# Four graph-attention layers on one core: new table rows stored from ScalarE's queue, and the smallest tile processed last

## The chip, the cores and the metric

The kernel runs on one core of a Trainium2 chip, with no other core at work. The metric is device time in microseconds, the median of repeated executions. One further execution was recorded by the hardware profiler; all durations, waits and times of day below come from that one. The engines are named as the profile names them: PE (TensorE), DVE (VectorE), ACT (ScalarE), POOL (GpSimd) and SP (SyncE), whose only work here is to issue transfers. PEld is the loading of weights into TensorE.

## The reference: what is computed

There are 3327 nodes with 512 features each, and one adjacency matrix with few entries. Four layers follow each other. Each normalises the rows of x (layer norm), applies ReLU, computes graph attention over the neighbours of every node, and adds the result to x:

```
h = relu(layernorm(x));  x = x + GAT_l(h, adj)          # l = 0, 1, 2, 3

GAT_l:  Wh = h @ W_l                                    # 512 -> 512, as 8, 4, 1, 8 heads
        s, d = Wh . a_src, Wh . a_dst                   # one number per node and head
        e[i, j] = leaky_relu(s[i] + d[j]), only where adj[i, j] > 0
        out[i] = sum_j softmax_j(e[i, :])[j] * Wh[j]    # elu on it in layers 1 and 2
```

## The kernel before

**Preparation.** The adjacency matrix is turned once into a list of neighbours for every node. Nodes are ranked by their number of neighbours and cut into 26 tiles of 128 nodes: tile 0 holds the nodes with the most neighbours, tile 25 those with the fewest. `CAPS` gives the number of neighbour slots of each tile: 36 for tile 0, 25 for tile 1, 23 for tile 2, 19 for tile 9, 12 for tile 24, 11 for tile 25. The lists themselves (`idxa` for tiles 18 to 25, `idxb` for the others) stay in SBUF.

**Tables.** For each layer there is a table in HBM with a row of 528 floats for each node: Wh and the attention numbers. Layer 0 reads `tabx`, made in the preparation. Later layers read `tabs[l % 2]` while they write `tabs[(l + 1) % 2]`, the table of the layer after.

**Steps.** A tile of a layer is done in steps of up to four slots (`GROUP`). For one step:
- `Tile.fetch` gathers one neighbour row for each of 128 nodes per slot, by an indirect DMA that POOL issues (L830, `g<-tab`). The node's own row is slot 0 and comes by a plain load from SP (L861); in layer 0 it comes with a gather of double width.
- `Tile.scored` computes the weights: two small operations on DVE (L883, L885, tile `z`), then Exp on ACT (L886, tile `pw`).
- `Tile.group` multiplies the four gathered rows by their weights on DVE (L912, tile `m`), and PE adds them up in PSUM (L917, tile `bank`, two matmuls per slot). In layer 2, with one head, DVE does both by itself (L905 and L907).

`steps` is the list of all steps of a layer, tile after tile in the order of the list `order`, which counts down from 25: the tile with the fewest slots comes first. Gathers are issued `LOOK` = 7 steps ahead. Tile indices below `DENSE[l]` (0, 1, 9 and 2 in the four layers) are left out of this list. They are done by dense attention over all nodes instead (classes `Several` and `Wholes`), in units that are spread evenly over the steps, up to eight before the last. Their loads (L1094, L1096, L1225, L1226) come from SP.

**The end of a tile.** After a tile's last step, `finish` and `ends` put the pieces that remain at fixed distances behind it: the divisors (L922 to L924), the mean (L934, in layer 2 L930), elu (`bent`, L940 and L942), the addition to x (L954), then for the next layer the centring (`xn`, L962, and its squares, L965), the root (L970, L435 to L441, in layer 2 on POOL, L432), the turn by four transposes (L451), ReLU (`hT`, L458), the projection of 16 matmuls (L469, tile `pv`, one PSUM buffer), and last `rows`: ACT copies the scaled result to `v` (L476, three buffers), and SP stores it in the next layer's table (L988, `tab<-v`). There are 78 such stores, one for each tile of layers 0 to 2.

**Order on the engines.** On PE, DVE, ACT and POOL the instructions stand in the order in which the code emits them; nothing passes a waiting instruction. On SP a scheduler sets the order of the transfers. The first gather of a layer waits until all rows of its table have been stored.

**The end of layer 0.** Between the last eight steps, and after them, stand 26 steps of class `Ranked`: each gathers mask rows (POOL, `spare<-found`) into one of three buffers and stores them again, sorted (SP, L1056, `masks<-spare`), for the dense parts of the later layers. Nine further steps of class `Mask` are inserted at fixed numbers earlier in layer 0. `Weights` loads a later layer's matrix (L394, `w<-in_w`, two transfers of 512 KB).

Of the kernel before, what the change touches and what calls it, by code (L numbers as in the profile page):

```python
# [18 lines left out]
P = 128  # L19
# [454 lines left out]
def scaled(nc, pv, rstd, work):  # L474
    v = work.tile([P, ROW], F32, name="v", bufs=3)
    nc.scalar.activation(v.rearrange("p (s n) -> p s n", s=2), pv[:, :, :ROW // 2], AF.Copy, scale=rstd)  # L476
    return v
# [47 lines left out]
def tile_gat_stack(ctx: ExitStack, tc: tile.TileContext, x, adj, adjT, ws, avs, out):  # L525
# [261 lines left out]
    with cond.Else():  # L787
        tile_gat_lists(tc, x, adj, ws, avs, out, ident, half, slots, L, low, spare, tabx, tabs)
# [3 lines left out]
def tile_gat_lists(ctx: ExitStack, tc: tile.TileContext, x, adj, ws, avs, out, ident, half, slots, L, low, spare, tabx, tabs):  # L792
# [7 lines left out]
    nc = tc.nc  # L800
    NP, F = x.shape
    NT = NP // P
# [32 lines left out]
    def scatter():  # L835
        while waiting:
            dst, t, rows = waiting.pop(0)
            nc.gpsimd.indirect_dma_start(out=dst, out_offset=bass.IndirectOffsetOnAxis(ap=slots(t, 0), axis=0),  # L838
                                         in_=rows, in_offset=None)

    class Tile:
# [143 lines left out]
        def rows(self):  # L985
            if self.W is not None:
                v = scaled(nc, self.pv, self.rstd, work)
                nc.sync.dma_start(tabs[(self.l + 1) % 2][self.t * P:(self.t + 1) * P, :], v)  # L988

        def ends(self, s):  # L990

# [54 lines left out]
    class Ranked:  # L1046
# [5 lines left out]
        def fetch(self):  # L1052
            n = ND * P // 4
            rows = spare[:, self.j % 3 * n:(self.j % 3 + 1) * n].bitcast(I32)
            gather(rows, found, slots(self.j, 0))
            nc.sync.dma_start(masks[:, self.j, :, :].rearrange("s p c -> p s c"),  # L1056
                              rows.rearrange("p (s c) -> p s c", c=wide // 4))
# [259 lines left out]
    def later(s, place, piece):  # L1317
# [2 lines left out]
    out_v = dram_disjoint_views(out, NT)  # L1320
    ctx.enter_context(tc.manual_schedule(engines={mybir.EngineType.Pool, mybir.EngineType.PE,
                                                  mybir.EngineType.DVE, mybir.EngineType.Activation}))
    order = list(reversed(range(NT)))
    ys = itertools.cycle([low[:, 3 * F:4 * F], low[:, 4 * F:5 * F]])
    W = None
    following = Weights(nc, wpool, work, 1, ws, avs)
# [112 lines left out]
```

## Time and profile before

| | |
|---|---|
| median of 3 runs | 2492.9 us (2492.3 to 2494.5) |
| the profiled execution, whole / its span | 2493.66 us / 2491.9 us |
| busy: PE, DVE, POOL, ACT | 2083.4, 1935.6, 1710.7, 911.6 us (84%, 78%, 69%, 37%) |
| gathers and scatters on POOL | about 0.95 us each |
| preparation ends, first steps of layer 0 | about 320 us |
| first gather of layer 1 | 944.5 us |
| first gather of layer 2 | 1502.0 us |
| first gather of layer 3 | 1966.4 us |
| last output scatter | 2483.9 us |

The busy times overlap: each is the time in which that engine worked, whatever the others did. What a layer costs is read from the engine that has no gaps in it, and what a boundary between layers costs is read from the time between the last gather of one layer and the first of the next. In lines of groups, "m<-g,pw" is the output tile and the inputs; "x1304 | 810.6, 681" is the number of instructions, their busy time in us and the mean duration of one in ns; behind the second bar stands how long the engine was idle just before them, and what ended that. In lines of the timeline the first number is the start and the second the duration, both in us; the bracket at the end holds the idle time before and what ended it.

### The profile page before, as it was taken

The page shows a single profiled execution, that of the slowest core. Times are in us where ns is not written, and L with a number is a line of the kernel's source. Part 1 is how long each engine was busy: PE and PEld are TensorE (multiplying, and loading weights), DVE is VectorE, ACT ScalarE, POOL GpSimd, SP SyncE. Part 2 cuts the span into 40 slices and gives each one's busy share as a digit, 9 for nine tenths or more (in the row PEclk, how much of TensorE's full clock was granted, in tenths as well). Part 3 has the DMA queues.
Part 4 walks back from the last instruction along what each step waited for, and adds up shares of the span by engine and source line. Part 5 has one row for each costly group of instructions (what it writes and reads, how often), then busy time and mean ns, then how long its engine had stood idle before and what let it go on. Part 6 is the DMA issues. An engine that isn't in the chain of part 4 may idle for free. (4 is left out here: it accounts for less than half of the span.)

```text
span 2491.9 us, 26810 instructions
## 1 busy us (share of the span) xinstructions
PE 2083.4 (84%) x6832; PEld 1163.5 (47%) x6832; DVE 1935.6 (78%) x5004; ACT 911.6 (37%) x2506; POOL 1710.7 (69%) x1700
## 2 busy tenths in 40 slices
PE   3776789999898855999999986869696699999897
PEld 1655445555444422555555543434353454455453
DVE  7887787887767735788888876978979488787776
ACT  4777123343321102433333323433333343333330
POOL 7798367777777756776777746655546377777775
PEclk9888899999999987999999998979898899999999
DMA  6797579999887777877888858867777488888885
GB/s 231 280 298 240 173 219 291 284 298 296 277 270 237 231 194 239 261 244 228 247 258 258 252 162 264 271 194 239 211 229 212 134 253 247 246 250 250 240 243 173
DMA packets 262490, 599.55 MB, mean 241 GB/s; under 512 B 103923, under 2 KB 121331, under 8 KB 257974
## 3 DMA queue, kind: packets, MB, share of 16 engines
q0 software_dynamic: 126128, 438.08, 57.7%
q1 hardware_dynamic: 132454, 152.86, 19.2%
q10 hardware_dynamic: 3744, 6.82, 0.8%
q8 instruction: 55, 0.90, 0.1%
q14 instruction: 109, 0.89, 0.1%
HBM read 547.96 MB, written 49.65 MB: 240 GB/s over the span
## 5 line engine op out<-in xcount | busy, mean ns | idle before, releaser
L917 PE MATMUL bank<-m,ident 128*128 128x512 f32 x2608 | 1204.6, 608 | 132.6 <-DVE m L912 132.0
L912 DVE TENSOR_TENSOR m<-g,pw 128x512 f32<-128x512 f32 x1304 | 810.6, 681 | 137.3 <-ACT pw L886 131.5
L830 POOL DMA_INDIRECT g<-tab,idxb x734 | 698.2, 951 | 284.7 <-issue 173.1
L917 PEld LDWEIGHTS bank<-m,ident 128*128 128x128 f32 x2608 | 483.3, 193 | 714.0 <-issue 347.5
L469 PE MATMUL pv<-w,hT 128*128 128x264 f32 x1664 | 438.5, 420 | 67.4 <-ACT hT L458 38.8
L886 ACT ACTIVATE pw<-z 128x32 f32<-128x32 f32 (+5 forms) x434 | 84.0, 194 | 987.2 <-DVE z L885 987.1
L469 PEld LDWEIGHTS pv<-w,hT 128*128 128x128 f32 x1664 | 340.3, 208 | 170.3 <-ACT hT L458 44.1
L830 POOL DMA_INDIRECT g<-tabx,twiceb x342 | 324.2, 948 | 105.1 <-issue 78.6
L830 POOL DMA_INDIRECT g<-tab,idxa x297 | 283.6, 955 | 145.1 <-issue 78.2
L1133 PE MATMUL whole<-ve,em 128*128 128x512 f32 x468 | 222.4, 623 | 41.4 <-DVE em L1119 38.5
L883 DVE TENSOR_TENSOR z<-g,pw 128x32 f32<-128x32 f32 (+5 forms) x434 | 74.9, 173 | 189.3 <-DMA g<-tab,idxa 83.0
L683 POOL TENSOR_TENSOR key<-a,keys 128x3328 int32<-128x3328 int32 (+1 forms) x29 | 189.1, 6525 | 14.5 <-DVE cand L692 11.8
L907 DVE SCALAR_TENSOR_TENSOR bank<-g,pw,bank 128x512 f32<-128x512 f32 x243 | 183.2, 754 | 6.8
L1133 PEld LDWEIGHTS whole<-ve,em 128*128 128x128 f32 x468 | 90.1, 199 | 152.3 <-issue 90.7
L692 DVE MAX8 cand<-key 128x8 f32<-128x208 int32 x416 | 143.7, 363 | 0.1
L830 POOL DMA_INDIRECT g<-tabx,twicea x99 | 94.4, 954 | 67.8 <-issue 32.7
L451 PE MATMUL pt<-ident,xn 128*128 128x128 f32 x416 | 68.6, 291 | 85.5 <-ACT hT L458 31.0
L451 PEld LDWEIGHTS pt<-ident,xn 128*128 128x128 f32 x416 | 53.6, 149 | 122.6 <-issue 48.4
L1108 ACT ACTIVATE r<-low,mc,b 128x384 f32<-128x384 f32 x78 | 52.6, 674 | 153.5 <-DVE em L1119 116.6
L432 POOL TENSOR_TENSOR rstd<-ve,half 128x1 f32<-128x1 f32 x52 | 31.8, 611 | 107.3 <-DVE ve L970 61.7
L1242 ACT ACTIVATE r<-low,spare 128x256 f32<-128x256 f32 x208 | 98.9, 476 | 5.1
L885 DVE SCALAR_TENSOR_TENSOR z<-z 128x32 f32<-128x32 f32 (+5 forms) x434 | 78.8, 182 | 15.3 <-DVE z L883 0.4
(175 smaller groups left out, 2111.5 us busy)
## 6 DMA issues: line engine op xcount, KB each, us to landing
a<-in_adj SPq DMA_DIRECT2D x25, 1664.0 KB, 9.0
tab<-v SPq DMA_DIRECT2D x78, 264.0 KB, 4.0
ve<-tab SPq DMA_DIRECT2D x78, 264.0 KB, 4.5
g<-tab SPq DMA_DIRECT2D x66, 264.0 KB, 4.7
tabx<-vx SPq DMA_DIRECT2D x26, 528.0 KB, 9.5
g<-tab,idxb POOLq DMA_INDIRECT x734, 3.9
low<-tab SPq DMA_DIRECT2D x52, 132.0 KB, 3.4
room<-tab SPq DMA_DIRECT2D x52, 132.0 KB, 3.6
```

What stands on the lines that cost most here:

```text
L451: nc.tensor.transpose(pt[:, k, :], xn[:, k * P:(k + 1) * P], ident)
L469: nc.tensor.matmul(pv[:, s, :HF + 8], hT[:, k, :], W.w[:, k, s, :], start=(k == 0), stop=(k == KC - 1))
L683: nc.gpsimd.tensor_tensor(key[:, c:c + quarter], a[:, c:c + quarter], keys[:, c:c + quarter], OP.mult)
L692: nc.vector.max(cand[:, g * 8:(g + 1) * 8], key[:, g * SEG:(g + 1) * SEG])
L830: nc.gpsimd.indirect_dma_start(out=out_, out_offset=None, in_=table, in_offset=bass.IndirectOffsetOnAxis(ap=which, axis=0))
L885: nc.vector.scalar_tensor_tensor(z, z, SLOPE, z, OP.mult, OP.max)
L886: nc.scalar.activation(self.wt[:, k0:k0 + n, :H], z, AF.Exp)
L907: nc.vector.scalar_tensor_tensor(acc, v, w, acc, OP.mult, OP.add)
L912: nc.vector.tensor_tensor(m[:, q, :].rearrange("p (s h d) -> p s h d", s=2, d=D), v.rearrange("p s (h d) -> p s h d", d=D), wt[:, k0 + q, ...
L917: nc.tensor.matmul(self.po, ident, m[:, q, :], start=(k0 + q == 0), stop=(k0 + q == K - 1))
L1133: nc.tensor.matmul(tl.po.rearrange("p (s m) -> p s m", s=2), e[:, q * P:(q + 1) * P], v.rearrange("p (s m) -> p s m", s=2)[:, :, :F // 2], ...
L1242: nc.scalar.activation(self.r[:, h, :], self.a[:, g, :], AF.Relu, bias=-1.0, scale=self.b[:, j, g:g + 1])
```

## The change

There are two edits. The store of the new rows is issued from ScalarE's queue, directly behind the instruction that makes `v`, in place of SP's. And the order of the tiles in every layer becomes 24, 23, ..., 0, 25: the tile with the fewest slots moves from the head of the list to its end. Tiles that are done densely in a layer are left out of it as before.

```diff
         def rows(self):
             if self.W is not None:
                 v = scaled(nc, self.pv, self.rstd, work)
-                nc.sync.dma_start(tabs[(self.l + 1) % 2][self.t * P:(self.t + 1) * P, :], v)
+                nc.scalar.dma_start(tabs[(self.l + 1) % 2][self.t * P:(self.t + 1) * P, :], v)
...
-    order = list(reversed(range(NT)))
+
+    order = [*reversed(range(NT - 1)), NT - 1]
```

## The prediction

> **What bounds the kernel now.** I read the group list first, then the busy times by stretch, the waits of POOL and SP, and last the timeline around each of the three places where one layer ends and the next begins.
>
> From the group list and the DMA issues of the page:
>
> ```profile
> L830 POOL DMA_INDIRECT g<-tab,idxb x734 | 698.2, 951 | 284.7 <-issue 173.1
> ...
> tab<-v SPq DMA_DIRECT2D x78, 264.0 KB, 4.0
> ```
>
> A gather takes 0.95 us of POOL and is followed by 0.30 us before the next: one neighbour row per node every 1.25 us. Busy time by stretch (columns: PE, PEld, DVE, ACT, POOL busy with counts, clock, DMA share, GB/s):
>
> ```profile
> 1200.00:1470.00 270.00, 265.30 (x834) 144.71 (x833) 231.49 (x617) 97.84 (x283) 202.40 (x214) 1.00 0.83 251
> 1470.00:1502.00 32.00, 23.39 (x73) 13.71 (x71) 13.26 (x42) 6.25 (x14) 0.02 (x1) 0.95 0.17 49
> 1502.00:1700.00 198.00, 148.84 (x420) 80.47 (x421) 161.01 (x301) 77.70 (x218) 120.95 (x128) 0.89 0.78 244
> ```
>
> 214 POOL instructions by 1.25 us are 267.5 of 270 us: late in layer 1 the gathers fill the time, with PE (265.3) close behind. Layers 0 and 3 look alike. In layer 2 DVE leads (161 of 198 us). Between layers POOL does nothing: the next layer's gathers read the whole table, so the first waits for the last new row. The waits, of all engines and of SP's queue (total, times, longest):
>
> ```profile
> POOL g L830 <- DMA tab<-v: 40.6, 2, 32.7
> ...
> SPq L988 <- ACT v L476: 444.4, 70, 28.4
> ```
>
> The three boundaries in the timeline; 0 to 1, then 1 to 2, then 2 to 3:
>
> ```profile
> 917.71 0.70 ACT L476 ACTIVATE v<-pv,rstd 128x528 f32<-128x528 f32 x1 [5.61 <-PE pv L469]
> ...
> 939.40 0.52 SPq L988 DMA_DIRECT2D tab<-v  x1
> ...
> 935.67 0.94 POOL L830 DMA_INDIRECT spare<-found,idxa  x1 [0.50 <-issue]
> 944.54 0.94 POOL L830 DMA_INDIRECT g<-tab,idxa  x1 [7.92 <-DMA tab<-v]
> ```
>
> ```profile
> 1487.29 0.70 DVE L934 TENSOR_TENSOR bank<-bank,den 128x512 f32<-128x512 f32 x1 [6.93 <-PE bank L917]
> ...
> 1498.38 0.70 ACT L476 ACTIVATE v<-pv,rstd 128x528 f32<-128x528 f32 x1 [5.35 <-PE pv L469]
> 1499.11 0.32 SPq L988 DMA_DIRECT2D tab<-v  x1
> ...
> 1501.98 0.94 POOL L830 DMA_INDIRECT g<-tab,idxa  x1 [32.69 <-DMA tab<-v]
> ```
>
> ```profile
> 1962.53 0.70 ACT L476 ACTIVATE v<-pv,rstd 128x528 f32<-128x528 f32 x1 [5.51 <-PE pv L469]
> ...
> 1966.37 1.00 POOL L830 DMA_INDIRECT g<-tab,idxa  x1 [9.51 <-issue]
> ```
>
> At 0 to 1 the last row is ready at 918.4 and leaves SP at 939.4, 21 us late: it stands behind eleven masks<-spare stores, each waiting for its own gather. At the other two it leaves within 0.1 us. So a new queue can shorten the first boundary only.
>
> **The skill.** "DMA: Bandwidth & Descriptors", section "Issuing engines are not separate DMA queues", says that another issuing engine saves only the sequencer's issue time. For the transfer the trace agrees (issue 0.32 us, median landing 4.0 us); but the 21 us are order in a queue, which that sentence leaves out. The same page, under "Anatomy of one DMA", puts every semaphore wait on the issuing sequencer; SP's 444.4 us agree, and that wait moves to ScalarE's stream.
>
> **The change part by part.**
>
> *Stores to ScalarE.* 78 issues leave SP, which then issues its loads and masks<-spare without waiting for v. ACT gets 78 issues. The row for ACT's own DMA (L711, set-up) has 0.335 us, plus 0.017 us for a semaphore: 78 x 0.35 = 27 us of ACT. Behind each stands the next pw (L886), for which the products of DVE (L912) wait. But v is emitted after the pw of its step, and in the layer 1 timeline ACT then idles 2.5 to 6 us before the next pw: I take 0 there. In layer 2, where DVE waits for ACT's r (29.5 us in 17 waits), the bound is 26 x 0.35 = 9 us; I take 0.5, for the tail. Below nothing: SP's loads come earlier, but no engine shows a wait of over 28 us in total for them, and the largest are the boundary's own; I take 0.
>
> The built order of the changed kernel shows a second wait. DMA completions share eight semaphores in turn, and a DMA waits for the last that used its semaphore. For stores within a layer that is mostly a transfer eight places back, in layer 1 about one tile (some 30 us) ago: landed. At the end of layer 0 it isn't: the store of tile 0 waits for masks<-spare number 14, that of tile 25 for number 22 (counted from 0). Number 14 is issued at 916.97 now and lands about 919.5; number 22 lands about 935.5, when gather number 25 gets its buffer (935.67).
>
> *Boundary 0 to 1.* ACT finishes v of tile 0 near 902, stands at its store until 919.5, and with it xn (0.7), the turn (0.7), hT (0.6 after the squares), the projection (5.5) and v (0.7) of tile 25, which stand behind it in ACT's order or need it: v at about 928.5. Its store waits until 935.5, then issue 0.35 and 2.1 us (the shortest landing of tab<-v): 938.0. POOL comes free at 936.6 from the 26 gathers of masks, an order that is unchanged, so the first gather of layer 1 stands at 938.2 for 944.54: **6.3 us gained**. The upper bound is 936.9 (7.6 us). The lower: w<-in_w, 2 x 512 KB, now starts with the gathers; at 298 GB/s, the best slice, it takes 3.5 us from them: 2.8 us.
>
> *Smallest tile last.* Tile 25 (11 slots, 3 steps: 10 gathers on POOL, in layers 1 to 3 one own-row load on SP, 11 products on DVE, 22 matmuls, a projection of 16 matmuls) moves from the head to the end of each layer, past the other tiles in POOL's and SP's queues. Counts stay, so the last gather stays; dense units, Mask and Ranked steps keep their step numbers. What moves is what lies behind the last gather.
>
> *Boundary 1 to 2.* Now the last tile has 25 slots, and the projection of the tile before (3.7 us, at 1482.7) stands in PE ahead of the last two matmuls: DVE waits 6.93 us. In the new order tile 2's projection comes eleven slots earlier and tile 1's after tile 25's matmuls. PE, near full here, then ends these about 1483.2, not 1487.25; the normalising on DVE starts 4 us earlier. Given back: tile 1's projection (3.7) lies between it and tile 25's turn, beside DVE's and ACT's 4 us, and ACT copies v and issues a store (1.05) before it can turn to hT of tile 25. **2.5 us gained**; bounds: loses 2 (both projections in a row) and gains 5 (a PE without backlog).
>
> *Boundary 2 to 3.* DVE is late, not PE: its last product ends at 1950.2 and then come 12.3 us to v. DVE's work is the same; four projections and tile 9's now press on one PSUM buffer, about 4.8 us each. v and store of tile 9 come before xn of tile 25 on ACT, ready at about 1954, when xn is due. **0.5 us lost** (the above); bounds +3 and -3, since the 3.3 us stall of DVE at 1932.6 may stay or go.
>
> *End.* The last tile's last group has 3 slots before (23) and after (11), and the output scatters run on POOL after the last gather either way: 0, bounds 1 us.
>
> Sum: 6.3 + 2.5 - 0.5 = 8.3 us off. The profiled execution took 2493.66 us (span 2491.9), 0.8 us above the median of 2492.9: 2485.4 there, 2484.6 for the median.
>
> **The rivals.** *The boundaries are hidden* (0.18): the start of layer 1 gains only 2.8 us because of the weights, the order gains nothing at the second boundary and the third loses 0.5: 2490.6, no change. For it: the weights load really is issued beside the first gathers, and PE at 265 of 270 us could be what layer 1 ends on. Against it: POOL's gathers fill that stretch just as well.
>
> *ScalarE's queue becomes the bound* (0.17), slower: in layer 2 the issue counts in full (9.1 us), and one store in each of layers 0, 1 and 2 waits for a load's landing (about 4.5 us each, 13.5) with pw behind it: 22.6 - 8.3 = 14.3 us slower, 2507. It decides from 13.3 us of such stalls on, 0.17 us for each of 78 stores. For it: ACT's order is written by hand and nothing passes a waiting store. Against it: ACT is busy 37% of the span.
>
> *The stores' move brings nothing*: if the last store waits for the masks to the end, number 25 (issued at 938.46, landed 2.1 us later), it leaves at 940.6, lands at 943.0 and gains 1.3 us: 2489.6, no change too; this shares the first rival's chance.
>
> **How the numbers follow.** The boundary gains carry 0.65. Changes within 0.2% (5 us, about what a measurement here can tell from none) are 2487.9 to 2497.9; the first rival falls there, 0.18; the second beyond, 0.17. Forecast 2484.6. Best bounds (7.6 + 5 + 3) give 2477.3, and 1 us at the end 2476; above, the range reaches past the first rival and part of the second, to 2499.
>
> **What would show it.** The first gather of layer 1 (idxa, after the last spare<-found) near 938 with a wait under 3 us; ACT idle some 17 us before xn in the tail of layer 0; the POOL gap of 32.7 us down by 2 to 3; the one before layer 3 (40 us without a gather) unchanged within 3; DVE's wait for pw, 131.5 us now, up by less than 10. The forecast is wrong if that wait grows by 15 us or more, if stores on ACTq show waits inside the layers, or if the second gap grows.

## The result, and the profile after

The changed kernel takes 2509.4 us (median of 6 runs, 2506.9 to 2515.0) where the kernel before takes 2492.9 (6 runs, 2489.9 to 2494.5): a ratio of 1.0070, with a 95% interval from 1.0057 to 1.0083. It is **16.5 us slower**; 8.3 us less were forecast. Its profiled execution took 2506.9 us, 2.5 below its own median, with a span of 2504.3, 12.4 more than before. The steps below are judged against these 12.4.

The group list and the DMA issues of the page of the changed kernel:

```profile
L830 POOL DMA_INDIRECT g<-tab,idxb x734 | 699.7, 953 | 285.3 <-issue 167.8
...
tab<-v ACTq DMA_DIRECT2D x78, 264.0 KB, 4.1
```

The gathers cost what they did, and so does a store, which lands 4.1 us after its issue where it took 4.0: the transfers are the same, now issued by ACT. Busy time by stretch of the changed kernel (columns as before: PE, PEld, DVE, ACT, POOL busy with counts, clock, DMA share, GB/s):

```profile
1200.00:1470.00 270.00, 262.42 (x813) 141.50 (x812) 227.72 (x613) 96.26 (x279) 198.86 (x210) 0.99 0.84 249
1470.00:1502.00 32.00, 26.81 (x95) 16.54 (x93) 15.39 (x45) 10.09 (x19) 0.00 (x0) 1.00 0.27 81
1502.00:1700.00 198.00, 151.61 (x421) 79.85 (x422) 161.45 (x301) 77.66 (x216) 122.36 (x131) 0.90 0.79 244
```

Late in layer 1 POOL still fills the time (210 instructions by 1.25 us are 262.5 of 270). In the second row more work stands behind the last gather than before: 95 matmuls where 73 stood, 10.1 us of ACT for 6.3. The waits of the changed kernel (total, times, longest):

```profile
POOL g L830 <- DMA tab<-v: 50.5, 3, 39.0
...
DVE ve L970 <- ACT waste L965: 40.8, 30, 5.5
...
ACT xn L962 <- DMA masks<-spare: 8.3, 1, 8.3
...
ACT neg L940 <- ACT v L476: 7.7, 19, 0.4
...
ACT xn L962 <- ACT v L476: 5.7, 14, 0.4
```

SP's 444 us of waiting for `v` are gone. The last two lines are new: 33 times ACT idles 0.4 us before `neg` or `xn`, because a store stands between it and `v`. The three boundaries in the timeline of the changed kernel, in the order of before. First 0 to 1:

```profile
909.26 0.70 ACT L476 ACTIVATE v<-pv,rstd 128x528 f32<-128x528 f32 x1 [6.55 <-PE pv L469]
917.94 0.33 ACTq L988 DMA_DIRECT2D tab<-v  x1
918.31 0.72 ACT L962 ACTIVATE xn<-x,nm 128x512 f32<-128x512 f32 x1 [8.35 <-DMA masks<-spare]
...
926.61 0.70 ACT L476 ACTIVATE v<-pv,rstd 128x528 f32<-128x528 f32 x1 [5.78 <-PE pv L469]
935.28 0.33 ACTq L988 DMA_DIRECT2D tab<-v  x1
```

For 8.35 us ACT stood at the first of these stores, which waited for a masks<-spare transfer, and `xn` stood behind it. The last store leaves ACT at 935.3, and the first gather of layer 1 stands at 939.29 (944.54 before). Then 1 to 2:

```profile
1477.14 0.70 ACT L476 ACTIVATE v<-pv,rstd 128x528 f32<-128x528 f32 x1 [5.70 <-PE pv L469]
1477.87 0.33 ACTq L988 DMA_DIRECT2D tab<-v  x1
1478.24 0.18 ACT L886 ACTIVATE pw<-z 128x12 f32<-128x12 f32 x1 [0.40 <-ACT v L476]
1478.45 2.48 DVE L912 TENSOR_TENSOR m<-g,pw 128x512 f32<-128x512 f32 x4 [4.23 <-ACT pw L886]
...
1488.39 0.69 DVE L934 TENSOR_TENSOR bank<-bank,den 128x512 f32<-128x512 f32 x1
...
1503.52 0.94 POOL L830 DMA_INDIRECT g<-tab,idxa  x1 [39.00 <-DMA tab<-v]
```

The last group's `pw` stands behind `v` and store of another tile, and DVE waits 4.23 us for it. The store is not what makes this wait: it is the same in the run order_again, which has the new order and leaves the stores on SP:

```profile
1477.36 0.70 ACT L476 ACTIVATE v<-pv,rstd 128x528 f32<-128x528 f32 x1 [6.22 <-PE pv L469]
1478.16 2.48 DVE L912 TENSOR_TENSOR m<-g,pw 128x512 f32<-128x512 f32 x4 [4.23 <-ACT pw L886]
```

`v` itself waits 5.7 or 6.2 us for its projection on PE, and `pw` stands behind it. And 2 to 3:

```profile
1949.66 0.33 ACTq L988 DMA_DIRECT2D tab<-v  x1
1950.04 0.63 ACT L940 ACTIVATE neg<-low 128x512 f32<-128x512 f32 x1 [0.40 <-ACT v L476]
1951.36 0.69 DVE L948 SCALAR_TENSOR_TENSOR low<-ex,low 128x512 f32<-128x512 f32 x1 [8.49 <-ACT ex L942]
```

Where DVE waited 3.3 us for an elu in the tail of layer 2 (the stall at 1932.6 that the prediction named), it now waits 8.5. Read off the first gather of each layer, the stages of all profiled executions that follow (us; the last stage ends with the span):

| kernel | to layer 1 | layer 1 | layer 2 | layer 3 and end | span |
|---|---|---|---|---|---|
| before | 944.5 | 557.4 | 464.4 | 525.5 | 2491.9 |
| changed | 939.3 | 564.2 | 470.9 | 529.9 | 2504.3 |
| both_again | 941.5 | 567.5 | 469.8 | 530.5 | 2509.4 |
| stores_again | 938.7 | 566.9 | 464.9 | 525.5 | 2496.1 |
| order_again | 947.8 | 554.6 | 466.5 | 530.3 | 2499.2 |
| layer0_stores | 945.7 | 559.6 | 462.0 | 526.8 | 2494.0 |
| late_stores | 939.1 | 558.6 | 464.3 | 525.4 | 2487.4 |
| late_both | 937.6 | 556.6 | 467.7 | 529.2 | 2491.0 |
| layer0_stores_layer1_order | 937.9 | 554.0 | 458.7 | 525.7 | 2476.2 |
| layer2_order | 945.2 | 557.7 | 466.1 | 525.3 | 2494.3 |
| layer3_order | 946.2 | 557.8 | 461.4 | 528.3 | 2493.7 |
| layer3_order_held | 946.9 | 556.1 | 464.5 | 527.1 | 2494.6 |
| late_stores_layer1_order | 939.5 | 555.8 | 463.6 | 525.5 | 2484.4 |

The changed kernel gains 5.3 us before layer 1 and loses 6.8, 6.5 and 4.3 in the three stages after. Layer 2 in its old order, stores directly behind `v` or not, took 458.7 to 464.9 us: a difference of 3 us in one stage of one execution decides nothing; medians do. Other stages that a kernel left as they were spread less: 944.5 to 946.9 for the start of layer 1 (stores on SP in layer 0), 556.1 to 559.6 for layer 1, 525.3 to 526.8 for the last.

### The profile page after: what moved, and what is told of

The parts are those of the page before. It is cut to its first block, busy times and chain, and to the rows that moved or that the text cites. A ratio compares the mean times of both kernels' runs of the same rounds, so it can differ in the third digit from the quotient of the medians.

```text
span 2504.3 us, 26800 instructions
## 1 busy us (share of the span) xinstructions
PE 2085.8 (83%) x6832; PEld 1162.8 (46%) x6832; DVE 1934.2 (77%) x5004; ACT 916.4 (37%) x2506; POOL 1711.8 (68%) x1700
## 4 chain that ended last, share of the span: by engine, by line
DVE 28%; PE 20%; DMA 18%; POOL 16%; issue 12%; ACT 6%; ACTq 0%; DVEq 0%; POOLq 0%; SPq 0%
DVE m L912 10%; PE bank L917 9%; POOL g L830 9%; DMA g<-tab,idxb 7%; POOL key L683 6%; PE pv L469 5%; DVE bank L907 3%; DMA g<-tab,idxa 3%; DMA g<-tabx,twiceb 2%; PE whole L1133 2%; DMA g<-tabx,twicea 1%; DVE z L885 1%; PE pi L781 1%; DVE z L883 1%; ACT pw L886 1%
## 5 line engine op out<-in xcount | busy, mean ns | idle before, releaser
L912 DVE TENSOR_TENSOR m<-g,pw 128x512 f32<-128x512 f32 x1304 | 810.7, 681 | 150.0 <-ACT pw L886 145.7
L469 PE MATMUL pv<-w,hT 128*128 128x264 f32 x1664 | 432.4, 416 | 63.5 <-ACT hT L458 38.8
L886 ACT ACTIVATE pw<-z 128x32 f32<-128x32 f32 (+6 forms) x434 | 83.9, 193 | 973.8 <-DVE z L885 970.6
L1133 PE MATMUL whole<-ve,em 128*128 128x512 f32 x468 | 228.1, 637 | 46.9 <-DVE em L1119 46.4
L883 DVE TENSOR_TENSOR z<-g,pw 128x32 f32<-128x32 f32 (+6 forms) x434 | 74.6, 172 | 169.8 <-DMA g<-tab,idxa 78.0
L885 DVE SCALAR_TENSOR_TENSOR z<-z 128x32 f32<-128x32 f32 (+6 forms) x434 | 78.7, 181 | 14.9
```

What stands on the lines that cost most here:

```text
L469: nc.tensor.matmul(pv[:, s, :HF + 8], hT[:, k, :], W.w[:, k, s, :], start=(k == 0), stop=(k == KC - 1))
L883: nc.vector.tensor_tensor(z, g[:, :n, ROW - 8:ROW - 8 + H], self.s.unsqueeze(1).to_broadcast([P, n, H]), OP.add)
L885: nc.vector.scalar_tensor_tensor(z, z, SLOPE, z, OP.mult, OP.max)
L886: nc.scalar.activation(self.wt[:, k0:k0 + n, :H], z, AF.Exp)
L912: nc.vector.tensor_tensor(m[:, q, :].rearrange("p (s h d) -> p s h d", s=2, d=D), v.rearrange("p s (h d) -> p s h d", d=D), wt[:, k0 + q, ...
L1133: nc.tensor.matmul(tl.po.rearrange("p (s m) -> p s m", s=2), e[:, q * P:(q + 1) * P], v.rearrange("p (s m) -> p s m", s=2)[:, :, :F // 2], ...
```

## The experiments

In brackets behind each time stand its ratio to the kernel before and the ratio's 95% interval. The ratio is not exactly the quotient of the two medians (late stores below: 0.9956, the medians give 0.9968; the interval holds both). Where whole times are subtracted, they are medians.

Seven of the runs fell on two chips where the kernel before takes 3003 or 2994 us: TensorE's mean granted clock was 0.87 to 0.88 there against 0.945, and PE was busy 2232 to 2250 us in place of 2083. Many semaphore records are missing in those traces, so only times are used from them. All the other runs compare with a kernel before of 2493.5 to 2494.7 us.

**The two halves, and twice the issues** (on the chip with the lower clock). The first kernel has only the edit at the store, the second only the edit of `order`. In the third the store is cut in two:

```diff
-                nc.sync.dma_start(tabs[(self.l + 1) % 2][self.t * P:(self.t + 1) * P, :], v)
+                tab = tabs[(self.l + 1) % 2]
+                nc.scalar.dma_start(tab[self.t * P:self.t * P + 64, :], v[:64, :])
+                nc.scalar.dma_start(tab[self.t * P + 64:(self.t + 1) * P, :], v[64:, :])
```

> Only the stores move to ScalarE's queue; the order of the tiles is that of before. Theory 1 (the order of the tiles is what costs): the first gather of layer 1 stands at about 939.5 instead of 944.5, POOL's gap before layer 2 stays at 32 to 34 us, the end is as before, and the whole is 5 to 6 us quicker than before, 2487 to 2488. Theory 2 (the issues and waits on ScalarE's queue cost): DVE's wait for pw grows by 12 us or more as in the changed kernel, and the whole is slower than before, 2497 to 2508.

> Only the order of the tiles changes; the stores stay on SP. Theory 1 (order): POOL's gap before layer 2 is about 38 us, the first gather of layer 3 comes 10 us or more later than before, the end costs some 4 us more, and the first gather of layer 1 is not earlier than 944; the whole is 2507 to 2514. Theory 2 (ScalarE's queue): none of this shows, the whole is within 3 us of before.

> Order of before, stores on ScalarE's queue, and each of them cut into two transfers of 64 rows, so that ScalarE issues 156 transfers in place of 78. Theory 1: the added 26 us of issue lie beside other work except at the tails and in layer 2; it stands within 4 us above the kernel with the stores alone moved. Theory 2: as much is lost again as the first 78 cost, 10 us or more above it.

Measured: stores alone 3004.7 against 3003.3 (1.0019, 0.9996 to 1.0043), order alone 2989.6 (0.9974, 0.9951 to 0.9998), doubled stores 3038.3 (1.0143, 1.0110 to 1.0176). The doubling costs 33.5 us over the single stores, 0.43 us for each of 78 more issues: it does not lie beside other work, as theory 1 had it. The order even gains on this chip. The theory that the order is all that costs falls here.

**The whole and its halves where before takes 2494.7 us**, and the stores of layer 0 alone:

```diff
-                nc.sync.dma_start(tabs[(self.l + 1) % 2][self.t * P:(self.t + 1) * P, :], v)
+                (nc.scalar if self.l == 0 else nc.sync).dma_start(tabs[(self.l + 1) % 2][self.t * P:(self.t + 1) * P, :], v)
```

> The changed kernel itself once more, beside its two halves on one chip, since the first three ran where the kernel before took 3003 us and not 2493. Both theories: 12 to 18 us slower than before where before takes 2493 us. Where before takes some 3000 us: theory 1 (order) has no reason for less than that; theory 2 (ScalarE's queue) has the sum of the two halves measured there, +0.2% and -0.3%, within 5 us of before.

> Stores on ScalarE's queue, order of before. Where before takes 2493 us, theory 1: 2487 to 2488, the first gather of layer 1 near 939.5 and no other part longer. Theory 2: 2497 to 2508, the loss inside the layers or at their ends, with DVE's wait for pw 12 us or more above 131.5. Where before takes some 3000 us: +0.2% as in the first run.

> Order changed, stores on SP. Where before takes 2493 us, theory 1: 2507 to 2514, POOL's gap before layer 2 near 38 us, the first gather of layer 3 some 10 us late, 4 us more at the end. Theory 2: within 3 us of before. Where before takes some 3000 us: -0.3% as in the first run.

> Order of before; ScalarE issues only the 26 stores of layer 0, SP those of layers 1 and 2. Theory 1: like all stores moved, 5 to 6 us quicker than before (2487 to 2488), since the gain is all at the boundary 0 to 1. Theory 2: quicker than all stores moved by two thirds of what these cost.

Measured: both 2511.8 (1.0057, 1.0038 to 1.0075); stores 2500.2 (1.0020, 1.0013 to 1.0028); order 2502.0 (1.0027, 1.0017 to 1.0036); stores of layer 0 alone 2490.6 (0.9977, 0.9967 to 0.9988). So each half costs, 5.5 and 7.3 us, and each theory held half. The two make 12.8 us, the whole 17.1; its interval (9.5 to 18.7 us) holds both. The stores of layer 0 gain 4 us; those of layers 1 and 2 then cost 9.5, and the stages put it into layer 1 (557.4 to 566.9). In its trace the order alone shortens layer 1 by 2.8 and lengthens the stage before it by 3.3, layer 2 by 2.1 and the end by 4.8. Only the end stands far outside what the stage takes where it is left as it was (3.5 us above the longest); layer 1 is settled below by more runs. (The profiled execution of layer0_stores was the slowest of its ten. Its first gather of layer 1 stands 0.30 us behind POOL's last mask gather, which ended late, at 945.3: there the masks set the time, not the store.) On DVE's wait for `pw` my theory 2 was off too: it grew by 26 us in stores_again, but 20 of them are one store of the end of layer 0 that waits for the masks, and most of the cost is not there.

Where in layer 1? I counted its 406 gathers along POOL's timeline. From the 91st to the 241st take 204.6 us before, 205.1 with only layer 0's stores on ACT, 210.0 with all of them there: the lead of 5.8 us is lost in a stretch in which PE is busy 194 of 205 us and gathers wait for buffers. The waits of that stretch, stores_again:

```profile
POOL g L830 <- DVE m L912: 18.7, 15, 3.6
...
DVE ve L970 <- ACT waste L965: 11.2, 6, 3.0
DVE bank L948 <- ACT ex L942: 3.8, 4, 2.0
ACT xn L962 <- ACT v L476: 2.8, 7, 0.4
ACT neg L940 <- ACT v L476: 1.6, 4, 0.4
```

and the kernel before, which has the last two of these lines not at all:

```profile
POOL g L830 <- DVE m L912: 13.5, 14, 2.9
...
DVE ve L970 <- ACT waste L965: 9.2, 6, 2.5
DVE bank L948 <- ACT ex L942: 2.7, 4, 1.4
```

DVE waits in its fixed order for the squares of `xn` (L970) and for the elu (L948), and both stand behind `v` and store of another tile on ACT. What comes late on DVE frees the buffers late for which POOL's gathers wait (18.7 us in place of 13.5). In the timeline of ACT, stores_again:

```profile
1072.74 0.68 ACT L476 ACTIVATE v<-pv,rstd 128x528 f32<-128x528 f32 x1
1073.45 0.33 ACTq L988 DMA_DIRECT2D tab<-v  x1
1073.83 0.72 ACT L962 ACTIVATE xn<-x,nm 128x512 f32<-128x512 f32 x1 [0.40 <-ACT v L476]
1074.58 0.63 ACT L965 ACTIVATE waste<-xn 128x512 bf16<-128x512 f32 x1
1075.12 0.19 ACT L965 ACTIVATION_READ_ACCUMULATOR waste<-xn 128x1 f32 x1
```

From the start of `v` to that of `xn` it is 1.09 us; without a store between them it is 0.59 (late_stores, below), so that `xn` begins 0.09 before `v` ends. A store directly behind `v` thus holds ACT for 0.50 us. Eleven of them are 5.5 us in a stretch that grew by 5.4, but the sizes alone prove nothing: ACT is busy 81 of 210 us there, and DVE's two waits grew by 3.1 us together. That the place of the store is the cause has to be tried.

**The store at the end of its step.** To test that, `v` stays in place and the store is issued after all else of the step, behind the neighbours' `xn`, `neg` and `ex`, once with the old order and once with the new one. Two further kernels go with them: layer 0's stores on ACT with the new order in layer 1 alone, and the new order in layer 3 alone (stores on SP).

```diff
+        def store(self):
+            if self.W is not None:
+                nc.scalar.dma_start(tabs[(self.l + 1) % 2][self.t * P:(self.t + 1) * P, :], self.v)
...
+                                    (b + 5 - (HEADS[self.l] == 1), "end", self.store),
...
                 do("last")
+                do("end")
```

```diff
+    last = [*order[1:], NT - 1]
...
-            tiles = [Tile(l, t, W) for t in order if t >= DENSE[l]]
+            tiles = [Tile(l, t, W) for t in (last if l in (1,) else order) if t >= DENSE[l]]
```

The kernels with the new order in another layer alone have that layer's number in place of the 1.

> Order of before, all stores on ScalarE's queue, but each issued at the end of its step, behind the centring (xn) and the elu (neg, ex) of the neighbouring tiles, and not directly behind v. Theory A (what the stores cost is the 0.73 us by which xn and neg stand later, for which DVE waits in its fixed order): DVE's waits for waste and ex in the middle of layer 1 fall back to those of before (9 and 3 us), the stretch from gather 90 to gather 240 of layer 1 takes 205 us again and not 210, and the whole is 2489 to 2492, 8 to 11 us under the kernel with the stores directly behind v (2500). Theory B (the issue costs wherever it stands on ScalarE): 2497 to 2502.

> The changed kernel with each store issued at the end of its step, as in the kernel late_stores. Theory A: the order alone cost 7 us and the stores give back 4, so 2497 to 2500, 12 to 15 us under the changed kernel. Theory B: 2509 to 2513, like the changed kernel.

> Stores on ScalarE's queue in layer 0 alone, and the smallest tile last in layer 1 alone. If the traces of the kernel with the new order alone are read rightly (layer 1 shortened by 2.8 us, layer 2 longer by 2, the end by 5, and 3 us at the start from SP's queue), this is 2486 to 2489, under both kernels. If the layers do not add up so, 2491 or more.

> Stores on SP as before; the smallest tile last in layer 3 alone. If the end costs what the traces show, by two scatters ahead of the last gathers on POOL and 22 matmuls in place of 14 behind the last gather: 4 to 5 us slower than before, all of it between the last gather and the end or in the last gathers. If the prediction's zero for the end holds and the loss comes from the layers ahead: within 1 us of before.

The 0.73 us in the first text is wrong: I had added the issue (0.33) to an idle time of 0.40 that contains it. Measured: late stores 2485.8 (0.9956, 0.9939 to 0.9973) and with the new order 2495.0 (1.0002, 0.9996 to 1.0009). The same 78 stores by the same engine thus cost 0.20% directly behind `v` and gain 0.44% at the end of the step (5.5 us lost and 7.9 gained, by medians); in the changed kernel the step's end takes the 0.57% away. In the timeline of ACT, late_stores (its store has line 991):

```profile
1071.77 0.68 ACT L476 ACTIVATE v<-pv,rstd 128x528 f32<-128x528 f32 x1
1072.36 0.71 ACT L962 ACTIVATE xn<-x,nm 128x512 f32<-128x512 f32 x1
1073.10 0.63 ACT L965 ACTIVATE waste<-xn 128x512 bf16<-128x512 f32 x1
1073.10 0.33 ACTq L991 DMA_DIRECT2D tab<-v  x1
1073.63 0.19 ACT L965 ACTIVATION_READ_ACCUMULATOR waste<-xn 128x1 f32 x1
```

`xn` follows `v` after 0.59 us, and the issue runs beside `waste`, whose accumulator is read 0.53 us after its start, as without a store beside it (0.54 in the block of stores_again). In the middle of layer 1 DVE's waits are back at 9.1 and 2.7 us, POOL's for DVE's products at 15.8, and the stretch takes 205.9. With the new order the same stretch takes 199.3 and 199.8 us with stores on SP or late (order_again, late_both), and 205.1 and 206.8 with stores directly behind `v` (the changed kernel, both_again). Theory A holds as to the place of the store, and theory B falls; but both times lie 2 to 3 us under A's ranges, so the late store gained more than A explains.

Layer 0's stores with the order of layer 1 alone: 2481.2 (0.9950, 0.9930 to 0.9969), 5 us under its expectation; its layer 2, which is that of before, happens to be the shortest of all (458.7). The order of layer 3 alone: 2495.9 (1.0008, 1.0000 to 1.0017), 2.2 us, less than the 4 to 5 expected. What it does there, POOL and DVE of layer3_order:

```profile
2461.78 0.99 POOL L838 DMA_INDIRECT out<-x,idxb  x1 [0.30 <-DMA g<-tab,idxa]
...
2470.63 0.94 POOL L830 DMA_INDIRECT g<-tab,idxa  x1 [0.30 <-issue]
2471.15 0.19 DVE L883 TENSOR_TENSOR z<-g,pw 128x32 f32<-128x32 f32 x1 [4.75 <-DMA g<-tab,idxa]
```

Two scatters stand ahead of the last seven gathers, and DVE waits 4.75 us for these.

**The remaining shares of the order.** The smallest tile last in layer 2 alone; the kernel layer3_order with its scatters two steps later; and late stores with the order of layer 1:

```diff
-                                    (b + 5, "last", scatter)]:
+                                    (b + (7 if self.l == 3 else 5), "last", scatter)]:
```

> Stores on SP as before; the smallest tile last in layer 2 alone. If the ends of the dense tiles, pressed into the last steps, cost what the traces with the new order show there (the stretch from the first gather of layer 2 to that of layer 3 at 466 to 471 us, where kernels with the old order have 459 to 465): 3 to 5 us slower than before. If the prediction's 0.5 us holds: within 1.5 us of before.

> As the kernel layer3_order, but every output scatter of layer 3 is issued two steps later, so that none stands between the last gathers on POOL. If the scatters ahead of the gathers are the cost of the end: the last gather 2.6 us earlier and 0 to 0.5 us over before, 2493.5 to 2494.5 where before has 2493.7. If it is the longer work of the last tile behind the gathers (22 matmuls, 11 products): 2495 to 2496, as there.

> All stores on ScalarE's queue at the end of their step, and the smallest tile last in layer 1 alone. If the late store costs nothing and the parts add up: 2479 to 2482, like the stores of layer 0 alone with this order (2481.2), and 4 to 6 us under late_stores. If the stores of layers 1 and 2 still cost something on ScalarE: 2484 or more.

Measured: layer 2 alone 2496.3 (1.0014, 1.0005 to 1.0023), 2.9 us; layer 3 with held scatters 2494.7 (1.0002, 0.9994 to 1.0011), 1.2 us above the median of before and 0.5 by the ratio. Held scatters leave the first to the last gather of layer 3 at 504.0 us, as before (504.1), where layer3_order has 505.3 and order_again 506.7, and DVE's wait falls:

```profile
2472.05 0.19 DVE L883 TENSOR_TENSOR z<-g,pw 128x32 f32<-128x32 f32 x1 [2.29 <-DMA g<-tab,idxa]
```

From the last gather to the last scatter it stays at 15.1 us (15.0 in layer3_order, 13.5 before). Both expected causes are there by the trace, the scatters ahead of the gathers and the longer work behind them; the medians' intervals overlap, so their shares in time are not settled. In layer2_order the tail of layer 2 shows this line,

```profile
1947.56 0.69 DVE L948 SCALAR_TENSOR_TENSOR low<-ex,low 128x512 f32<-128x512 f32 x1 [8.06 <-ACT ex L942]
```

as in the changed kernel, without a store on ACT: it is the order's doing. The wait is 8.0 to 8.5 us in all five kernels with the new order in layer 2, and 1.6 to 3.3 in the eight others of the table. Late stores with the order of layer 1 took 2486.7 (0.9973, 0.9963 to 0.9982), no better than late stores alone, though its layer 1 is 2.8 us shorter. By its expectation that means that late stores in layers 1 and 2 still cost something; late stores alone do not show it. The parts do not add up there, and why is open.

Of the kernels of the table, ten have the stores of layer 1 on SP or late. From the first to the last gather of layer 1, the four with the new order take 518.4 to 519.2 us, the six with the old one 521.3 to 525.0. Nearly all of that lies in the stretch from the 91st to the 241st gather: 199.3 to 200.3 us against 202.7 to 205.9.

**Layers 0 and 1, and the two best once more** (these four again on a chip with the lower clock). Layers 0 and 1 have the new order alone, with stores on SP.

> Stores on SP as before; the smallest tile last in layer 0 alone. The order alone costs 7.3 us, of which layers 2 and 3 measured 2.9 and 2.0 and layer 1 seems to gain 2.8 by its trace. If the layers add up, layer 0 costs about 5: 2497 to 2500 where before has 2493.5, the first gather of layer 1 at 947 to 949. If they do not add up: within 2 us of before.

> Stores on SP as before; the smallest tile last in layer 1 alone. By the trace of the kernel with the new order alone, layer 1 takes 554.6 us and not 557.4, as the prediction's second step had it (2.5): 2490 to 2492 where before has 2493.5. If what it gains there is lost in layer 2: 2493 to 2495.

> Stores of layer 0 on ScalarE's queue and the smallest tile last in layer 1 alone, once more, since only four runs of it were compared: 2480 to 2484 if the 0.995 holds. If the late stores with the same order (2486.7) show the true sum: 2485 to 2488.

> All stores on ScalarE's queue at the end of their step, order of before, once more, since only four runs of it were compared: 2485 to 2487 if the 0.9956 holds; 2489 to 2491, like the stores of layer 0 alone, if the later position brings nothing beyond them.

Measured against 2994.4: the order in layer 0 alone 3008.0 (1.0049, 1.0026 to 1.0071), in layer 1 alone 2973.1 (0.9929, 0.9900 to 0.9957), layer 0's stores with the order of layer 1 2972.5 (0.9925, 0.9907 to 0.9944), late stores 2990.4 (0.9971, 0.9951 to 0.9990). The times expected do not apply to this chip, but the signs do: layer 0's order costs, layer 1's gains. The times of gathers can be read in these traces too: layer 1 takes 711.4 us with its new order alone and 729.4 with the new order in layer 0 alone, so the gain is in layer 1. The fastest version where before takes 2493.7 is layer 0's stores on ScalarE with the new order in layer 1 alone, 12.5 us under it, though by only four runs. Where before takes 2994.4 it is 21.9 us under it, by twenty runs, and cannot be told from the order of layer 1 alone (21.3 us). It is faster than both kernels of the case; the changed one took 2509.4.

## Why the prediction was wrong

The forecast of 2484.6 missed; the time lies above its range. The likeliest case had its sign wrong: the cost of a store on ScalarE inside the layers was put at nothing (0.5 us for the tail of layer 2), and measured 9.5 us; and the order was taken to gain 2 us, and cost 7.3. By steps:

- **Boundary 0 to 1: right.** Predicted first gather 938.2; it came at 939.3, and at 938.7 to 941.5 in the runs with all stores directly behind `v`. POOL was free at 936.9 (936.6) and waited for the last store, as forecast; the 1.1 us missing are this store's way from issue to gather, 4.0 us and not 2.7. (With the old order, in stores_again, POOL's mask gathers end last and set the time.) The last `v` was ready at 927.3 (predicted 928.5) and its store left at 935.3 (935.5). ACT stood 8.35 us before `xn`, not 17, because tile 0's `v` came at 909 and not at 902; that is off the path, since the last store's wait for the masks decides.
- **Stores inside the layers: the step that failed most.** "Behind each stands the next pw (L886) [...] I take 0 there." The bound of 27 us was drawn, but the value taken from the wrong neighbour. In the timeline of the kernel before, `xn` or `neg` of another tile stands directly behind `v` in 43 of the 78 cases and `pw` in 16 (37 and 18 in the changed kernel), and DVE's fixed order waits for them. Measured: 9.5 us for layers 1 and 2, by medians, and as far as single traces tell nearly all in layer 1 (566.9 us, against 556.1 to 559.6 with the old order and the stores of that layer on SP or late); put behind these instructions, with the old order, the stores cost nothing that can be seen. Layer 2, where the prediction looked for the cost, took 464.9 us in stores_again, within the spread of its old order.
- **Boundary 1 to 2: right in size for the order alone, by luck, and wrong in place.** 2.5 us were to come behind the last gather, where PE would be free earlier; "Counts stay, so the last gather stays" fails. In order_again the gathers of layer 1 take 518.9 us, not 523.8, and the gap behind them 35.8, not 33.6. With stores behind `v` the gap is 40.0: PE did not end early (1487.4, not 1483.2), and the last `pw` stands behind two copies of `v`, which wait for PE. It comes 14.7 us after the last gather, and 11.3 in order_again. The tile has left the crowded first half of the layer for the end, where POOL leads; that this is the reason was only argued, though the gain itself was measured (0.71% on the chip with the lower clock) and lies in the middle of the layer.
- **Boundary 2 to 3: too small.** 0.5 us taken, bound 3; the order of layer 2 alone measured 2.9 (1.2 to 5.7 by the ratio's interval), and with the stores the stage is 5.4 to 6.5 longer in two executions. It was not `v` and store of tile 9 before `xn` of 25 that decided, but hT and `v` of the dense tiles ahead of an elu earlier on ACT, for which DVE waits 8 us. Whether order and direct stores together cost more than their sum in this stage (469.8 and 470.9 us, against 466.1 to 467.7 with the new order alone or late stores) is not settled.
- **End: wrong.** "The output scatters run on POOL after the last gather either way": two moved ahead of it. 0 taken, bound 1; the order of layer 3 alone measured 2.2 (0 to 4.2 by the ratio's interval), and the traces show 2.8 to 5.0 with it.
- **SP's loads at 0: nothing seen against it** in the runs. The new order in layer 0 was given no cost of its own. With the stores on SP it costs 0.49% on the chip with the lower clock (on the others one trace has the first gather at 947.8, against 944.5 to 946.9); with the store on ACT no such cost shows at the first gather.

For the changed kernel's 12.4 us: -5.3 (predicted -6.3), +6.8 (-2.5), +6.5 (+0.5) and +4.3 (0). In layer 1 the 9.5 us of the stores and the -2.8 of the order make 6.7.

The Trainium skill's sentence in "DMA: Bandwidth & Descriptors", section "Issuing engines are not separate DMA queues", that another engine saves only issue time, again fits the transfer (4.0 and 4.1 us). What these runs add is the place: 0.50 us for whatever stands directly behind on ACT.

Of the rivals, "ScalarE's queue becomes the bound" came within 2.4 us of the time (2507), but not by its mechanism: its 9.1 us in layer 2 did not show, and stores of the changed kernel that themselves wait were seen at the end of layer 0 alone (three, of 2.8, 8.0 and 8.0 us). Of the signs named as fatal one came true: the second gap grew from 32.7 to 39.0. The gap before layer 3, to stay within 3 us, grew from 41.6 to 54.9. DVE's wait for `pw`, fatal from 15 us above 131.5 on, stayed just under (145.7), and was the wrong gauge: late_stores, faster than before, has 155.1. DVE's wait for `waste` rose from 25.4 to 40.8.

## What to carry to other kernels

When a DMA is moved to a computing engine, ask which instruction stands directly behind it and who waits for that one, not what the next critical instruction of the same tile is; issue it a few instructions later, behind those for which others wait. When work changes places in a fixed order, list what each in-order queue now has ahead of the last critical item (here two scatters before the last gathers, and `v` before the last `pw`), layer by layer: one order need not suit all.

## What the runs showed of the hardware

A store issued directly behind the activation that makes its data held ACT for 0.50 us (1.09 in place of 0.59 from `v` to `xn`), more than its issue of 0.33. Put behind `xn` and `waste`, it delayed neither: it was issued while `waste` ran. A store that waited for another transfer held ACT for the whole of that wait: 8.35 us before `xn` at the end of layer 0, for a masks<-spare transfer of SP.

The same kernel took 2493 us on some chips and 3003 or 2994 on others, where TensorE was granted 0.87 of its clock and not 0.945, and the same edit of the order had the opposite sign there (-0.26%, against +0.27%). With the stores alone moved, PE was busy 169 us longer on such a chip (2246.9 against 2078.0), and the span was 511 us longer (3006.7 against 2496.1): even if every added microsecond of PE lengthened the whole, that would be a third of it. What the rest is, these traces do not show.
